# A GINE layer loop in which the adjacency is built in turns, the node chain has empty steps, and the edge weights have one buffer

## The chip, the core and the metric

The kernel runs on one core of a Trainium2 chip. The metric is device time in microseconds (us) from the start to the end of one launch; shown is the median of several runs. Engines: PE multiplies matrices (PEld is its weight load), DVE and ACT do elementwise work, POOL issues the indirect gathers, SP issues most other DMAs. Each engine runs its instructions in order.

## What is computed

A network of four graph layers, each followed by a feed-forward layer, on 1875 nodes with 256 features. The change touches the first graph layer, GINE, which itself has four layers:

```python
def _gine(x, src, dst, edge_attr, W1, b1, W2, b2, eW, eb, eps):
    e = edge_attr @ eW + eb
    m = jax.nn.relu(x[src] + e)
    agg = jax.ops.segment_sum(m, dst, num_segments=N)
    h = (1.0 + eps) * x + agg
    return jax.nn.relu(h @ W1 + b1) @ W2 + b2
...
h = _gine(x, src, dst, edge_attr, W1[0], ...)
for k in range(1, L):
    y = jax.nn.relu(_layernorm(h, gamma[k], beta[k]))
    h = h + _gine(y, src, dst, edge_attr, W1[k], ...)
return jax.nn.relu(_layernorm(h, gamma[0], beta[0]))
```

There are 31875 edges, sorted by destination. While GINE runs, the kernel also builds the weighted adjacency matrix that a later graph layer (the third) multiplies with.

## The kernel before, in words

Nodes lie in 15 tiles of 128. The edges of a tile are a window of 18 columns of 128 edges (the last tile: 12). Two columns make an **item**, so there are 9 items per tile, 6 in tile 14, 132 per layer and 528 in all; they are numbered 0 to 527, and g131 below is the DVE addition of item 131.

For each item `fast_gine` records: two gathers of source rows by POOL (`gather`, L1081); the edge product on PE (`edges`, L572, into one of four PSUM banks, with the weights `ew`); the membership matrix s on DVE (`members`, L579); the addition of the product to the gathered rows on DVE and the relu on ACT (`messages`, L587 and L588); and two products s x m that add up a tile's sum on PE (`sums`, L601). Gathers are recorded 9 items ahead of the sums, edge products 5, messages 2. Gathers cannot cross into the next layer, since they read the table `qt` that the node chains of the layer write.

The **node chain** of a finished tile (`fast_gine_node`) is a generator in pieces: z on DVE (L691); two transposes on PE (L700); zT on ACT (L702); the product with W1 on PE (L708); uT on ACT (L712); the product with W2 on PE (L717); x, its statistics and the root (L721 to L729); the reciprocal, scale and relu (L1139 to L737); and the row of the next table with its DMA (L743, L744). One piece of each open chain is recorded per item (`node_work`), two per item in tile 14. With the last item of a layer all open chains are run to their end, and then the chain of tile 14 is recorded in one go, with some steps of the adjacency between its pieces (the tuple `more`). Only when its row has landed can the next layer's gathers start.

The **adjacency** is also a generator. The edges are in 120 groups of 16 destinations, three products each, two groups to a pair, so 60 pairs and 360 products. A product needs a one-hot `row` and a weighted one-hot `col` from DVE (L371, L374); its sum `padj` is in one PSUM bank (L378). A copy on ACT (L381) moves a pair's result to `adj_stage`, and every fourth pair SP writes that out (L385). `advance` takes one step; a credit `due` grows by `rate` per item from item 66 on, in tiles 0 to 12. `group_columns` prepares the columns of a third of the groups at three tiles; it first brings the adjacency to the end of a pair.

`gine_weights` loads the weights of a layer into a pool of two buffers, the next layer's at tile 2. `group_loads` and `prepare_experts` are chores, one per item; they bring POOL the iotas f2own and f3own, each followed by a memset on DVE (L1614, L1616).

Almost all of this is recorded through `self.later`, which keeps the engines' instructions in the order of the program; some loads and memsets are free and are placed by the scheduler.

Of the kernel before, what the change touches and what calls it, by code (L numbers as in the profile page):

```python
# [94 lines left out]
class Net:  # L95
# [261 lines left out]
    def adjacency(self, pools):  # L357

        nc, pin = self.nc, self.later
        for pair in range(NG // 2):
            t, q = divmod(2 * pair, GP)
            if q == 0:
                self.adj_stage = pools["st"].tile([P, NT, P], F32, name="adj")
            pa = pools["ad"].tile([P, 2, GN * NT], F32, name="padj")
            for i in range(2):
                for u in range(GT):
                    c = (2 * pair + i) * GT + u
                    row = pools["r"].tile([P, P], F32, name="row")  # L370
                    pin(nc.vector.tensor_scalar(row, self.iota, self.grow[:, c:c + 1], None,  # L371
                                                op0=ALU.is_equal))
                    col = pools["c"].tile([P, GN * NT], F32, name="col")
                    pin(nc.vector.tensor_scalar(col, self.wide, self.gcol[:, c:c + 1],  # L374
                                                self.gwt[:, c:c + 1], op0=ALU.is_equal,
                                                op1=ALU.mult))
                    yield "rows"
                    pin(nc.tensor.matmul(pa[:, i, :], row, col, start=u == 0, stop=u == GT - 1))  # L378
                    if u < GT - 1 or i == 0:
                        yield "sum"  # L380
            pin(nc.scalar.copy(  # L381
                self.adj_stage[:, :, q * GN:(q + 2) * GN].rearrange("p a (i n) -> p i n a", i=2),
                pa.rearrange("p i (n a) -> p i n a", a=NT)))
            if q == GP - 2:
                nc.sync.dma_start(self.adj[t], self.adj_stage)  # L385
            yield "pair"

    def window_attrs(self, one, starts):
        nc = self.nc
# [90 lines left out]
    def fast_layer0_gnn(self):  # L480
        nc, tc, a = self.nc, self.tc, self.a
        with ExitStack() as ctx:
            one = ctx.enter_context(tc.tile_pool(name="q1", bufs=1))
            wp = ctx.enter_context(tc.tile_pool(name="qw", bufs=2))
            y = one.tile([P, NT, D], F32, name="y")
            self.adj = self.dram.tile([NT, P, NT, P], F32, name="adj")
            self.wide = one.tile([P, GN * NT], F32, name="wide")
            nc.gpsimd.iota(self.wide, pattern=[[1, GN * NT]], base=0, channel_multiplier=0,
                           allow_small_or_imprecise_dtypes=True)
            h = one.tile([P, NT, D], F32, name="hres")  # L490
            tables = [self.dram.tile([NP, D], F32, name=f"qt{l}") for l in range(4)]
            ebs = []
            for l in range(4):
                ebs.append(self.vector_row(one, a["L0_gnn_eb"][l], f"eb{l}"))
            with tc.tile_pool(name="qn", bufs=1) as sb:
                self.layernorm(y, self.x, sb)
                t0 = sb.tile([P, NT, D], F32, name="tab0")
                nc.vector.tensor_tensor(t0, y, ebs[0][:, None, :].to_broadcast([P, NT, D]),
                                        ALU.add)
                nc.sync.dma_start(by_tile(tables[0]), t0)  # L500
            starts = self.windows()
            w = self.gine_weights(0, wp)
            pools = {
                "g": ctx.enter_context(tc.tile_pool(name="qg", bufs=10)),
                "m": ctx.enter_context(tc.tile_pool(name="qm", bufs=4)),
                "s": ctx.enter_context(tc.tile_pool(name="qs", bufs=4)),
                "r": ctx.enter_context(tc.tile_pool(name="qr", bufs=4)),
                "e": ctx.enter_context(tc.tile_pool(name="qe", bufs=2)),
                "pe": ctx.enter_context(tc.tile_pool(name="qp", bufs=1, space=PSUM)),
                "pa": ctx.enter_context(tc.tile_pool(name="qa", bufs=2, space=PSUM)),  # L510
                "mm": ctx.enter_context(tc.tile_pool(name="qx", bufs=1, space=PSUM)),
                "ad": ctx.enter_context(tc.tile_pool(name="qd", bufs=1, space=PSUM)),
                "st": ctx.enter_context(tc.tile_pool(name="qt", bufs=1)),
                "c": ctx.enter_context(tc.tile_pool(name="qc", bufs=4)),
            }
            self.window_attrs(one, starts)
            with tc.tile_pool(name="gc", bufs=1) as sb:
                self.group_rows(one, sb, pools["ad"])
            pools["gc"] = ctx.enter_context(tc.tile_pool(name="gk", bufs=1))
            self.fast_gine(y, h, tables, ebs, w, wp, pools)  # L520

    def gine_weights(self, l, wp):
        nc, a = self.nc, self.a
        nxt = (l + 1) % 4
        w = {
            "w1": self.weight(wp, a["L0_gnn_W1"][l], "w1"),
            "w2": self.weight(wp, a["L0_gnn_W2"][l], "w2"),
            "b1": self.vector_col(wp, a["L0_gnn_b1"][l], D, "b1"),
            "b2": self.vector_row(wp, a["L0_gnn_b2"][l], "b2"),
            "eps": self.vector_row(wp, a["L0_gnn_eps"][l:l + 1], "eps", 1),  # L530
            "gam": self.vector_row(wp, a["L0_gnn_gamma"][nxt], "gam"),
            "bet": self.vector_row(wp, a["L0_gnn_beta"][nxt], "bet"),
        }
        nc.vector.tensor_scalar(w["eps"], w["eps"], 1.0, None, op0=ALU.add)

        ew = wp.tile([P, 4, D], F32, name="ew")
        nc.vector.memset(ew, 0.0)
        for i in range(4):
            nc.sync.dma_start(ew[i * ED:(i + 1) * ED, i, :], a["L0_gnn_eW"][l])
        w["ew"] = ew  # L540
        return w

    def fast_gine(self, y, h, tables, ebs, w, wp, pools):

# [21 lines left out]
        def edges(q):  # L566
            l, t, k = items[q]
            i = k % 4 if k < 8 else t % 4
            at = self.attr[:, t, k // 4 * 2:] if k < 8 else self.tail[:, t // 4]
            pes[q] = pools["pe"].tile([P, 2, D], F32, name=f"pe{q % 4}")  # L570
            for v in range(2):
                pin(nc.tensor.matmul(pes[q][:, v, :], at[:, v, :], ws[l]["ew"][:, i, :],  # L572
                                     start=True, stop=True))

        def members(q):
# [31 lines left out]
        state = {"g": 0, "m": 0, "e": 0, "at": "pair", "due": 0.0}  # L607


        FIRST, BETWEEN = 66, 22  # L610
        shares = [q >= FIRST and t < NT - 2 for q, (l, t, k) in enumerate(items)]
        rate = (2 * NG * GT - 3 * BETWEEN) / sum(shares) + 0.01

        def advance():
            if state["at"]:
# [12 lines left out]
                messages(state["m"])  # L628
                state["m"] += 1

        def multiplied(to):

            while state["e"] < min(to, total, state["m"] + 4):
                edges(state["e"])
                state["e"] += 1

        multiplied(AHEAD)
        made(MADE, 0)
        multiplied(AHEAD)
        nodes = []  # L640

        def node_work(pieces=1):
# [6 lines left out]
        for q, (l, t, k) in enumerate(items):  # L649
# [9 lines left out]
            end = sums(q)  # L659
            last = end and t == NT - 1  # L660
            if last:
                node_work(99)
                node = self.fast_gine_node(l, t, accs.pop(t), y, h, tables, ebs, ws[l], pools)
                more = (0, 2, 0, 4, 0, 0, 0, 0, 16) if l < 3 else ()
                for n, _ in itertools.zip_longest(more, node):
                    for _ in range(n or 0):
                        advance()
            multiplied(q + 1 + AHEAD)
            gathers(q + 1 + GATHERS, l + 1 if last else l)
            made(q + 1 + MADE, l + 1 if last else l)  # L670
            state["due"] += rate * shares[q]
# [10 lines left out]
    def fast_gine_node(self, l, t, acc, y, h, tables, ebs, w, pools):  # L682


        nc, pin = self.nc, self.later
        sb, ps = pools["e"], pools["mm"]
        if l == 0:
            pin(nc.vector.tensor_scalar(self.deg[:, t:t + 1], acc[:, D:D + 1], 1.0, None,
                                        op0=ALU.add))
# [9 lines left out]
        for c in range(KD):  # L699
            pin(nc.tensor.transpose(pz[:, c, :], z[:, c * P:(c + 1) * P], self.ident))  # L700
        yield True
        pin(nc.scalar.copy(zT, pz))  # L702
        yield True
        p1 = ps.tile([P, KD, P], F32, name="mm")
        uT = sb.tile([P, KD, P], F32, name="uT")
        for m in range(KD):
            for kc in range(KD):
                pin(nc.tensor.matmul(p1[:, m, :], w["w1"][:, kc, m * P:(m + 1) * P], zT[:, kc, :],  # L708
                                     start=kc == 0, stop=kc == KD - 1))
        yield True  # L710
        for m in range(KD):
            pin(nc.scalar.activation(uT[:, m, :], p1[:, m, :], AF.Relu, bias=w["b1"][:, m:m + 1]))  # L712
        yield True
# [2 lines left out]
        for kc in range(KD):  # L716
            pin(nc.tensor.matmul(p2, uT[:, kc, :], w["w2"][:, kc, :], start=kc == 0,  # L717
                                 stop=kc == KD - 1))
        yield True
        x = h[:, t, :]  # L720
        pin(nc.vector.tensor_tensor(x, skip if l else w["b2"], p2, ALU.add))  # L721
# [1416 lines left out]
```

## Time and profile before

| | us |
|---|---|
| median of 7 runs | 3782.39 (3777.95 to 3785.62) |
| the profiled execution | 3781.21 |
| its span in the profile | 3779.4 |
| GINE: first gather starts | 69.35 |
| GINE: x of the last tile done | 1513.83 |
| busy over the span: PE, DVE, ACT, POOL | 2923.5, 1836.3, 885.0, 1528.8 |

How to read it: busy times are of the whole span, so they mix eight layers with different limits. The page's groups give, for a line of the kernel, an engine and an operation, how often it ran, the busy time, the mean of one, and the idle time of the engine just before with what ended it. "issue" there means that the profile shows nothing that the engine waited for. The timeline gives start, duration, engine, line, operation, output and inputs, and in brackets the idle time before and its end. Ends of matmuls are modelled.

### The profile page before, as it was taken

The page shows a single profiled execution, that of the slowest core. Times are in us where ns is not written, and L with a number is a line of the kernel's source. Part 1 is how long each engine was busy: PE and PEld are TensorE (multiplying, and loading weights), DVE is VectorE, ACT ScalarE, POOL GpSimd, SP SyncE. Part 2 cuts the span into 40 slices and gives each one's busy share as a digit, 9 for nine tenths or more (in the row PEclk, how much of TensorE's full clock was granted, in tenths as well). Part 3 has the DMA queues.
Part 4 walks back from the last instruction along what each step waited for, and adds up shares of the span by engine and source line. Part 5 has one row for each costly group of instructions (what it writes and reads, how often), then busy time and mean ns, then how long its engine had stood idle before and what let it go on. Part 6 is the DMA issues. An engine that isn't in the chain of part 4 may idle for free. (4 is left out here: it accounts for less than half of the span.)

```text
span 3779.4 us, 42835 instructions
## 1 busy us (share of the span) xinstructions
PE 2923.5 (77%) x14099; PEld 2406.4 (64%) x14099; DVE 1836.3 (49%) x4981; ACT 885.0 (23%) x1933; POOL 1528.8 (40%) x1537
## 2 busy tenths in 40 slices
PE   3878789989987998679456565939967999686992
PEld 2667678868776876457344454728855888574772
DVE  5556567757766775861357661061251111442224
ACT  1333233323332333213111110200111222011220
POOL 2777477757775776000578721020003111003220
PEclk9989899999999999789667666969977999886996
DMA  5435685434443333015444413412004554503663
GB/s 150 123 112 178 177 190 131 120 106 120 120 120 105 113 113 99 24 52 158 123 132 139 132 54 118 138 71 114 1 8 165 176 168 143 200 1 126 187 193 104
DMA packets 302412, 453.64 MB, mean 120 GB/s; under 512 B 91737, under 2 KB 230436, under 8 KB 300388
## 3 DMA queue, kind: packets, MB, share of 16 engines
q1 hardware_dynamic: 226324, 248.21, 21.0%
q0 software_dynamic: 72672, 199.68, 18.4%
q10 hardware_dynamic: 3184, 2.91, 0.2%
q8 instruction: 114, 1.87, 0.2%
q14 instruction: 118, 0.97, 0.1%
HBM read 363.11 MB, written 87.56 MB: 119 GB/s over the span
## 5 line engine op out<-in xcount | busy, mean ns | idle before, releaser
L1081 POOL DMA_INDIRECT g<-qt,w_src x1056 | 1026.6, 972 | 416.1 <-issue 306.4
L601 PE MATMUL acc<-m,s 128*128 128x256 f32 (+1 forms) x2112 | 555.0, 386 | 8.7 <-ACT m L588 8.7
L587 DVE TENSOR_TENSOR g<-g,pe 128x512 f32<-128x512 f32 x528 | 361.5, 685 | 340.0 <-DMA g<-qt,w_src 336.3
L572 PE MATMUL pe<-ew,w_attr 128*128 128x256 f32 x1888 | 497.1, 387 | 31.2 <-DVE g L587 22.4
L588 ACT ACTIVATE m<-g 128x512 f32<-128x512 f32 x528 | 333.1, 631 | 753.0 <-DVE g L587 467.2
L1081 POOL DMA_INDIRECT g<-rq_h,w_tsrc x264 | 301.3, 1141 | 390.7 <-PE pz L859 310.9
L601 PEld LDWEIGHTS acc<-m,s 128*128 128x128 f32 x2112 | 400.5, 195 | 56.7 <-ACT m L588 10.6
L572 PEld LDWEIGHTS pe<-ew,w_attr 128*128 128x128 f32 x1888 | 360.1, 194 | 102.3 <-PE acc L601 37.4
L1087 POOL DMA_INDIRECT f_outs<-ye,token x104 | 99.7, 959 | 508.7 <-DVE ye L1772 502.5
L996 PE MATMUL acc<-h,adj 128*128 128x256 f32 x1350 | 294.7, 379 | 0.0
L1763 PE MATMUL hid<-xeT,w 128*128 128x256 f32 x1184 | 272.4, 387 | 24.3 <-DVE xeT L1758 22.7
L378 PE MATMUL padj<-col,row 128*128 128x240 f32 x720 | 218.3, 392 | 84.7 <-DVE col L374 77.2
L996 PEld LDWEIGHTS acc<-h,adj 128*128 128x128 f32 x1350 | 255.6, 190 | 33.6
L1087 POOL DMA_INDIRECT f_slots<-rows,slot x60 | 57.6, 961 | 515.5 <-DVE sl L1698 301.8
L1769 PE MATMUL out<-w,hidT 128*128 128x256 f32 x1184 | 264.0, 379 | 0.0
L1763 PEld LDWEIGHTS hid<-xeT,w 128*128 128x128 f32 x1184 | 222.3, 193 | 63.2 <-DVE xeT L1758 31.5
L1765 ACT ACTIVATE hidT<-hid,cols 128x256 f32<-128x256 f32 x296 | 138.2, 473 | 459.4 <-PE hid L1763 459.4
L1769 PEld LDWEIGHTS out<-w,hidT 128*128 128x128 f32 x1184 | 225.4, 190 | 30.1
L579 DVE TENSOR_TENSOR s<-iota,w_dst 128x256 f32<-128x256 f32 x528 | 221.6, 420 | 20.5 <-PE acc L601 20.4
L378 PEld LDWEIGHTS padj<-col,row 128*128 128x128 f32 x720 | 135.3, 198 | 131.7 <-DVE col L374 83.7
L1772 DVE TENSOR_SCALAR ye<-out,xe 128x256 f32<-128x256 f32 x104 | 50.3, 484 | 253.7 <-PE out L1769 253.7
L374 DVE TENSOR_SCALAR col<-wide,g_col,g_wt 128x240 f32<-128x240 f32 x360 | 148.1, 411 | 0.0
(388 smaller groups left out, 3736.5 us busy)
## 6 DMA issues: line engine op xcount, KB each, us to landing
w<-in_L_ffn_W SPq DMA_DIRECT2D x44, 1024.0 KB
adj<-adj SPq DMA_DIRECT2D x45, 960.0 KB
w<-in_L_ffn_w SPq DMA_DIRECT2D x60, 512.0 KB
w<-in_L_ffn_w SPq DMA_DIRECT2D x18, 1024.0 KB
g<-qt,w_src POOLq DMA_INDIRECT x1056, 2.8
dstrow<-lin SPq DMA_DIRECT2D x14, 1152.0 KB
rq_h<-hr SPq DMA_DIRECT2D x8, 1980.0 KB
xe<-f_slots SPq DMA_DIRECT2D x52, 258.0 KB
```

The source lines that it names most:

```text
L374: pin(nc.vector.tensor_scalar(col, self.wide, self.gcol[:, c:c + 1], self.gwt[:, c:c + 1], op0=ALU.is_equal, op1=ALU.mult))
L378: pin(nc.tensor.matmul(pa[:, i, :], row, col, start=u == 0, stop=u == GT - 1))
L572: pin(nc.tensor.matmul(pes[q][:, v, :], at[:, v, :], ws[l]["ew"][:, i, :], start=True, stop=True))
L579: pin(nc.vector.tensor_tensor(ss[q], self.iota[:, None, :].to_broadcast([P, 2, P]), self.wdst[:, c:c + 2, None].to_broadcast([P, 2, P]), A ...
L587: pin(nc.vector.tensor_tensor(g, g, pes.pop(q), ALU.add))
L588: pin(nc.scalar.activation(m[:, :, :D], g, AF.Relu))
L601: pin(nc.tensor.matmul(accs[t], s[:, v, :], m[:, v, :], start=k == v == 0, stop=end and v == 1))
L996: nc.tensor.matmul(acc, adj[t][:, u, :], h[:, u, :], start=u == 0, stop=u == NT - 1)
L1081: self.nc.gpsimd.indirect_dma_start(out=out, out_offset=None, in_=table, in_offset=bass.IndirectOffsetOnAxis(ap=at, axis=0))
L1087: return self.nc.gpsimd.indirect_dma_start(out=table, out_offset=bass.IndirectOffsetOnAxis(ap=at, axis=0), in_=in_, in_offset=None, **kw)
L1763: nc.tensor.matmul(p1, w1[:, kc, m * P:(m + 1) * P], xT[:, kc, :], start=kc == 0, stop=kc == KD - 1)
L1769: nc.tensor.matmul(p2, hT[:, m, i * P:(i + 1) * P], w2[:, m, :], start=m == 0, stop=m == fc - 1)
```

## The change

The adjacency is written as a list of turns: per pair six products, a copy, and an empty turn (None). A step of the generator is now one turn. In turn n the row and column for turn n+2 are recorded first, then the product, the copy, or nothing. So rows and columns are two turns ahead of their product, and the copy stands in a turn of its own behind the sixth product. A step was half of that before (rows and column, or product), so `BETWEEN` falls from 22 to 11 and `rate` is worked out from 8 turns a pair.

The node chain has four empty pieces: ahead of z, ahead of zT, ahead of uT, and ahead of x. It has 13 pieces instead of 9, and the tuple `more` follows.

The edge weights `ew` lie in one buffer for all layers instead of one of two; it is set to zero once, the next layer's weights are loaded with the last item of a layer, and edge products no longer cross into the next layer ahead of its start. The pools of messages (`qm`) and membership matrices (`qs`) have 5 and 6 buffers instead of 4 each.

```diff
 def adjacency(self, pools):
+        def rows(i):
+            row = pools["r"].tile([P, P], F32, name="row")
+            pin(nc.vector.tensor_scalar(row, self.iota, self.grow[:, i:i + 1], None,
+                                        op0=ALU.is_equal))
+            col = pools["c"].tile([P, GN * NT], F32, name="col")
+            pin(nc.vector.tensor_scalar(col, self.wide, self.gcol[:, i:i + 1], self.gwt[:, i:i + 1],
+                                        op0=ALU.is_equal, op1=ALU.mult))
+            sides[i] = row, col
+        turns = []
         for pair in range(NG // 2):
...
+            turns += [(pair, u) for u in range(2 * GT)] + [(pair, "copy"), None]
+        for n, turn in enumerate(turns):
+            for m in (0, 1, 2) if n == 0 else (n + 2,):
+                if m < len(turns) and turns[m] and turns[m][1] != "copy":
+                    rows(turns[m][0] * 2 * GT + turns[m][1])
+            if turn:
...
+                if u == "copy":
...
+                    pin(nc.scalar.copy(
...
+                    row, col = sides.pop(pair * 2 * GT + u)
+                    pin(nc.tensor.matmul(pa[:, u // GT, :], row, col, start=u % GT == 0,
+                                         stop=u % GT == GT - 1))
+            yield "sum" if turn else "pair"
 def fast_layer0_gnn(self):
+            self.ew = one.tile([P, 4, D], F32, name="ew")
+            nc.vector.memset(self.ew, 0.0)
+            self.edge_weights(0)
...
-                "m": ctx.enter_context(tc.tile_pool(name="qm", bufs=4)),
-                "s": ctx.enter_context(tc.tile_pool(name="qs", bufs=4)),
+                "m": ctx.enter_context(tc.tile_pool(name="qm", bufs=5)),
+                "s": ctx.enter_context(tc.tile_pool(name="qs", bufs=6)),
 def gine_weights(self, l, wp):
-        ew = wp.tile([P, 4, D], F32, name="ew")
-        nc.vector.memset(ew, 0.0)
+    def edge_weights(self, l):
         for i in range(4):
-            nc.sync.dma_start(ew[i * ED:(i + 1) * ED, i, :], a["L0_gnn_eW"][l])
+            self.nc.sync.dma_start(self.ew[i * ED:(i + 1) * ED, i, :], self.a["L0_gnn_eW"][l])
 def fast_gine(...):
-        FIRST, BETWEEN = 66, 22
+        FIRST, BETWEEN = 66, 11
-        rate = (2 * NG * GT - 3 * BETWEEN) / sum(shares) + 0.01
+        rate = (NG // 2 * (2 * GT + 2) - 3 * BETWEEN) / sum(shares) + 0.01
-            while state["e"] < min(to, total, state["m"] + 4):
+            while state["e"] < min(to, total, state["m"] + 4) and items[state["e"]][0] <= layer:
...
             if last:
+                if l < 3:
+                    self.edge_weights(l + 1)
                 node_work(99)
...
-                more = (0, 2, 0, 4, 0, 0, 0, 0, 16) if l < 3 else ()
+                more = (0, 0, 1, 0, 0, 2, 0, 0, 0, 0, 0, 0, 8) if l < 3 else ()
...
-            multiplied(q + 1 + AHEAD)
+            multiplied(q + 1 + AHEAD, l + 1 if last else l)
 def fast_gine_node(...):
+        yield True
...
```

In the last function `yield True` is added ahead of z, between the transposes and zT, between the product with W1 and uT, and between the product with W2 and x.

## Prediction

> **What bounds the kernel.** I read, in this order: the page's costliest groups, who POOL waits for, a table of busy time in stretches of 30 us, and the timeline at the ends of GINE's four layers. The change touches this stage alone (its first gather starts at 69.35 us, its last tile is done at 1513.83 us of a span of 3779.4). Columns of the groups: busy us, mean ns of one | idle us before them and what ended most of it.
>
> ```profile
> L1081 POOL DMA_INDIRECT g<-qt,w_src x1056 | 1026.6, 972 | 416.1 <-issue 306.4
> ...
> L378 PE MATMUL padj<-col,row 128*128 128x240 f32 x720 | 218.3, 392 | 84.7 <-DVE col L374 77.2
> ```
>
> A gather takes 0.972 us and 0.30 us pass before the next: 1056 x 1.27 = 1343 us of a stage of 1444. The wait list of the gathers agrees: apart from that gap (306.4 us in 940 cases) only `DMA qt<-row` stops POOL for long, twice for 55.1 us together. The stretches (us, then busy us and count of PE, PEld, DVE, ACT, POOL, clock, DMA share, GB/s) show the trap:
>
> ```profile
> 540.00:570.00 30.00, 30.00 (x151) 26.87 (x150) 21.66 (x62) 11.08 (x22) 22.69 (x25) 1.00 0.42 110
> ...
> 960.00:990.00 30.00, 28.38 (x136) 24.41 (x135) 22.58 (x67) 11.05 (x21) 22.69 (x25) 1.00 0.46 143
> ```
>
> PE is busy all the time and POOL for 22.7 of 30 us, but the 25 gathers with 25 gaps of 0.30 us fill POOL's 30 us. PE is full because it lags and catches up. The gather of item i+10 waits for the ACT pass (L588) of item i; by the timeline there are usually 20 us between the two, and the least is 0.4 us (item 144: pass ends 496.1, gather 496.5). So inside a layer POOL is never held, whatever PE waits for. POOL stands only where one layer's table must be complete before the next layer's first gather:
>
> ```profile
> 405.87 0.63 POOL L1614 IOTA f2own<- 128x88 f32 x1
> 439.22 1.22 POOL L1081 DMA_INDIRECT g<-qt,w_src  x1 [32.73 <-DMA qt<-row]
> ...
> 777.16 0.94 POOL L1081 DMA_INDIRECT g<-qt,w_src  x1 [0.30 <-issue]
> 800.46 0.94 POOL L1081 DMA_INDIRECT g<-qt,w_src  x1 [22.35 <-DMA qt<-row]
> ...
> 1135.84 0.95 POOL L1081 DMA_INDIRECT g<-qt,w_src  x1 [0.30 <-issue]
> 1157.68 0.94 POOL L1081 DMA_INDIRECT g<-qt,w_src  x1 [20.90 <-issue]
> ```
>
> The stage is thus four runs of gathers (336.5, 338.9, 336.3, 338.0 us) and four tails: 33.4, 22.4, 20.9, and 18.1 us from the last gather's end (1495.70) to x of tile 14 (1513.83); together 1444.5. A change gains or loses in the tails, or not at all.
>
> How a tail runs, in layer 1's (P1, P2: products with W1, W2, L708 and L717; x: L721; z: L691):
>
> ```profile
> 780.92 0.69 DVE L587 TENSOR_TENSOR g<-g,pe 128x512 f32<-128x512 f32 x1 [1.97 <-DMA g<-qt,w_src]
> ...
> 781.77 0.91 DVE L537 MEMSET ew<- 128x1024 f32 x1 [0.16 <-DVE g L587]
> ...
> 782.60 0.36 DVE L721 TENSOR_TENSOR hres<-skip,mm 128x256 f32<-128x256 f32 x1
> ...
> 786.77 0.48 DVE L691 SCALAR_TENSOR_TENSOR z<-y,eps,acc 128x256 f32<-128x256 f32 x1
> ...
> 790.16 0.96 ACT L381 COPY adj<-padj 128x480 f32<-128x480 f32 x1 [2.00 <-PE padj L378]
> ...
> 792.76 0.42 DVE L721 TENSOR_TENSOR hres<-skip,mm 128x256 f32<-128x256 f32 x1 [2.03 <-PE mm L717]
> ```
>
> The last message is added at 780.92. Then DVE ends **tile 13's** chain (x at 782.60 to its row), and only behind it, in order, comes z of tile 14 at 786.77, though its last sum ended at 785.34. From z to x takes 5.99 us, from x to the next gather 7.7.
>
> **Part by part.**
>
> *Adjacency in turns.* No instruction is added: 360 rows, 360 columns, 720 matmul records, 60 copies stay. PE's waits for columns (161.0 us before matmul and weight load, 115 times) and for copies (23.5) should go. Price 0: the gathers hide them. Were that cover not there, 184.5 us would be the most to win.
>
> *Buffers for messages and members.* s waits 20.4 us for sums; same cover, 0.
>
> *Edge weights in one buffer.* Three memsets (0.91 us) go; the one at 781.77 stands just before x (its gain is in the sums below, which count from the old times). A layer's four ew loads stay four, but now wait for the old layer's last edge product (about 413 in layer 0), with SP's later issues behind them; the row of tile 14 is due over 15 us after that, so nothing. New: the next layer's first four edge products stand on PE behind the tail, not before it. They take 4 x 0.86 = 3.4 us (twice that if slow); the first gathered pair lands 1.25 + 0.95 + 2.8 = 5.0 us after its gather starts, and a delay beyond that meets the 20 us of slack. Price 0; without that cover up to 2 us at each of three boundaries.
>
> *Empty steps.* The chain of a tile has 13 pieces instead of 9. In tile 14 two run per item, over five items and a flush. So before, tile 13's P2 stands behind the third-last sum (PE order P2, sum 261, 262, 263) and tile 12's chain is over; after, P2 stands behind sum 262, x and all behind it in the flush, and tile 12's x and row lie between DVE's last additions. With the rows of the trace, layer 1:
> - g260 772.45, x to ve of tile 12 1.25 us, z and skip of 13 0.9, g261 775.5 (data at 775.32), rs, y, relu, row of 12 3.3 us to 778.85, g262 779.15 (data 777.93), its ACT pass to 780.55, zT to 780.95.
> - P1 of 13 1.0 start to start, sums 261 and 262 0.86 each, P2 1.13: ends 784.8; x 784.85, and x to z is as before (786.77 - 782.60 = 4.2): z at 789.05, **+2.3**.
> - PE is idle from 776.1 (sum 260) to 780.95. After gaps of 5.77 and 7.35 us PE began slow (407.78: 2.04 us instead of 1.03; 449.98: 2.08), and at 1494.34 P1 took 2.07 instead of 1.16 after 1.83 us. With P1 and the next sum at that pace 1.45 more: **+3.75**.
>
> The same sum gives +3.75 or +5.2 for layer 2 (data at 1131.46, 1133.69, 1136.43, 1139.53; z was at 1144.36) and +2.55 or +4.2 for layer 3 (1490.07 to 1498.36; z was at 1504.09, and P1 was slow there already).
> In layer 0, worked out in the same way, DVE waits 12.19 us for POOL's f2own iota, queued behind the layer's last gather, and is let go at 406.57, with 8 additions left; after with 6 (the memset is in front of g126), and no next-layer edge products on PE. But P2 of 12 and 13 hang on ACT passes behind it: P2(12) ends 410.9, z(13) 412.7, row(12) 415.5, g131 417.4, zT(13) 417.7, P1 418.9, two sums, P2(13) 421.35, x 421.4, z 4.3 later: 425.7. Before: 425.69. **0**: what the shorter queue gains goes into tile 13's chain.
>
> *The copy's place in the tail.* Before, a copy (0.96 us) stood on ACT between zT and uT in layers 1 and 2: z to x 5.99 and 6.39 us against 4.47 in layer 0 without one. After, the instruction order has it in layer 0 alone. There it starts when the product behind P1 ends, 0.45 us after P1, and uT 0.77 us later (as 790.16 and 790.93 show) instead of 0.03 after P1: **+1.2**; in layers 1 and 2 **-1.5** and **-1.9**. In layer 0 SP issued the last row 0.5 us late behind gam and bet, which now stand behind it: **-0.5**.
>
> *POOL's pace.* 170 gathers take over 0.99 us; over 0.946 all take 29.0 us more, 5.8 to 8.5 a layer, in step with what DVE does beside them. DVE's work stays and shifts: bounds +-5 (four times about half that spread), value 0.
>
> **Sum**, PE slow at the start of P1(13): 0 + 1.2 - 0.5 + (3.75 - 1.5) + (5.2 - 1.9) + 4.2 = **+10.4 us**; at full pace 5.9. I take the first, since the gaps (4.7 to 4.9 us) lie nearer 5.77 than the gaps that began at full pace (787.31: 1.97). If the last chain's P1 and P2 run slow too (PE idles some 4 us before z), 1.85 us more in each tail, 7.4 at most.
>
> [...]
>
> The profiled execution took 3781.21 us (1.8 around its span), 1.2 below the median of 7: 3781.2 + 10.4 + 1.2 = 3792.8; I say **3792.5**.
>
> **Rivals.**
> 1. *Nothing to measure*, within 0.2% (7.6 us, about what a measurement of this kernel can tell): PE starts P1(13) at full pace (+5.9), or POOL's pace gives some back: 3775 to 3790, most likely 3788. For it: at 1132.59 PE took the usual 0.44 us after 2.03 idle. 0.31.
> 2. *Faster*: tile 13's chain does not hold z of tile 14, because its P2 ends over 4.2 us before the last sum of tile 14. Then layer 0's tail wins (two additions and five edge products fewer behind the f2own wait: last ACT pass 418.3, sum 419.3, against 425.7: -6.4), the copies' 0.7 - 1.5 - 1.9 count in full, and the other z stay: -9.1, 3773.7. Against it: PE's order has P2(13) directly before that last sum. 0.07.
> 3. *PE was the bound*, so that its waits count: up to -184, 3598. Against: POOL's gaps of 0.30 us. 0.02.
> 4. *POOL held at item 144*, where the slack was 0.4 us: two more rows are flushed there. But PE no longer waits for the column at 481.88, and ends sum 140 earlier. Some 5 us more, 3797. 0.05.
> 5. *The change does not do what it says*: the order has rows two products ahead, so it does; no gain follows.
>
> Forecast 0.55. Slower 0.55 + 0.05 = 0.60, same 0.31, faster 0.07 + 0.02 = 0.09. The range: upwards all chains slow and POOL 5 us worse, 10.4 + 7.4 + 5 = 22.8 over 3782.4, 3805; downwards rival 1's lower part, 3776, where rival 2 begins.
>
> **What would show it.** Runs of gathers at 336 to 339 us each (else POOL's pace or rival 4); PE's waits for columns and copies near none while the stage does not shorten; tails near 34.1, 24.6, 24.2 and 22.3 us; tile 14's z directly behind tile 13's row; P1 of tile 13 near 2 us. A tail of layer 0 under 29 us, or tails 1 to 3 not longer, would prove it wrong.

## The result, and the profile after

The changed kernel takes 3794.66 us (median of 13 runs) where the kernel before takes 3782.39 (33 runs): a ratio of 1.0033, 95% interval 1.0026 to 1.0040, or 12.3 us more. The forecast was 3792.5 us.

Three groups of the page of the changed kernel answer to those shown before (busy us, mean ns of one | idle us before them and what ended most of it):

```profile
L1101 POOL DMA_INDIRECT g<-qt,w_src x1056 | 1024.4, 970 | 428.5 <-issue 346.0
...
L396 PE MATMUL padj<-col,row 128*128 128x240 f32 x720 | 207.5, 384 | 15.7 <-DVE col L369 12.8
...
L396 PEld LDWEIGHTS padj<-col,row 128*128 128x128 f32 x720 | 142.2, 200 | 38.4 <-ACT adj L386 10.5
```

The weight loads of the kernel before:

```profile
L378 PEld LDWEIGHTS padj<-col,row 128*128 128x128 f32 x720 | 135.3, 198 | 131.7 <-DVE col L374 83.7
```

The change did what it says: PE's idle time ahead of the adjacency products fell from 84.7 to 15.7 us, that ahead of their weight loads from 131.7 to 38.4. The two overlap and must not be added: the time in which neither ran fell from 84.2 to 15.6 us. The gathers did not notice: 1024.4 us busy instead of 1026.6, and 12 us more idle.

The idle time is in the tails, as the timeline of POOL in the changed kernel shows:

```profile
405.10 0.63 POOL L1634 IOTA f2own<- 128x88 f32 x1
439.30 0.96 POOL L1101 DMA_INDIRECT g<-qt,w_src  x1 [33.56 <-DMA qt<-row]
...
806.44 0.94 POOL L1101 DMA_INDIRECT g<-qt,w_src  x1 [27.39 <-issue]
...
1169.81 0.94 POOL L1101 DMA_INDIRECT g<-qt,w_src  x1 [26.63 <-issue]
```

With the end of the stage that makes the table below (us). z, x and next are the sections of a tail: from the last gather's end to the start of tile 14's z, from there to the end of its x, from there to the next gather (in layer 3, to the end of the tile's work).

| tail | before | after | more | z | x | next |
|---|---|---|---|---|---|---|
| layer 0 | 33.36 | 34.20 | +0.8 | +0.5 | +2.4 | -2.1 |
| layer 1 | 22.36 | 27.40 | +5.0 | +4.9 | 0.0 | +0.2 |
| layer 2 | 20.89 | 26.63 | +5.7 | +5.0 | +0.7 | +0.1 |
| layer 3 | 18.13 | 23.17 | +5.0 | +3.8 | +1.2 | +0.1 |
| sum | 94.74 | 111.40 | **+16.7** | +14.1 | +4.3 | -1.7 |

The four runs of gathers take 336.18, 339.74, 336.74 and 335.69 us, together 1.4 less than before; the first gather starts 0.4 earlier, and the unchanged code behind the stage took 3.9 us less in this execution. That makes 10.9 us between the two spans (3790.3 and 3779.4).

Layer 1's tail in the timeline of the changed kernel (its last gather ended at 779.04):

```profile
779.23 0.43 DVE L763 TENSOR_TENSOR row<-y,eb 128x256 f32<-128x256 f32 x1 [0.48 <-ACT y L757]
...
780.75 0.63 ACT L602 ACTIVATE m<-g 128x512 f32<-128x512 f32 x1 [1.55 <-DVE g L601]
781.28 0.35 ACT L720 COPY zT<-mm 128x256 f32<-128x256 f32 x1
781.69 2.08 PE L726 MATMUL mm<-zT,w 128*128 128x128 f32 x8 [4.61 <-ACT zT L720]
...
783.56 3.62 PE L615 MATMUL acc<-m,s 128*128 128x256 f32 x8
...
786.97 1.35 PE L736 MATMUL mm<-w,uT 128*128 128x256 f32 x4
...
788.36 0.42 DVE L741 TENSOR_TENSOR hres<-skip,mm 128x256 f32<-128x256 f32 x1 [5.59 <-PE mm L736]
...
792.25 0.43 DVE L763 TENSOR_TENSOR row<-y,eb 128x256 f32<-128x256 f32 x1 [0.48 <-ACT y L757]
792.59 0.47 DVE L708 SCALAR_TENSOR_TENSOR z<-y,eps,acc 128x256 f32<-128x256 f32 x1
...
793.12 0.44 PE L717 MATMUL mm<-ident,z 128*128 128x128 f32 x2 [3.93 <-DVE z L708]
...
794.02 1.71 PE L726 MATMUL mm<-zT,w 128*128 128x128 f32 x8
```

Tile 12's row (779.23) stands on DVE in front of the last additions; zT of tile 13 waits on ACT behind the pass of one of them (780.75); so P1 of tile 13 starts only at 781.69, after 4.61 us of idle PE, and takes 2.08 us; in the kernel before it took 1.16 (at 777.11). The two sums behind it take 1.81 each, where one took 1.03. P2 ends, x of tile 13 follows at 788.36, its row at 792.25, and directly behind it z of tile 14 at 792.59, 13.55 us after the last gather instead of 8.67. In the kernel before, too, z stood directly behind the end of tile 13's chain, but only 0.1 to 1.5 us after tile 14's last sum; now it is 3.4 to 3.5 us after it in all four layers, and in layers 1 to 3 that sum itself ends 1.8 to 2.9 us later after the last gather. Then PE has been idle for 3.93 us again, and P1 of tile 14 takes 1.71 instead of 1.05.

### The profile page after: what moved, and what is told of

The parts are those of the page before. It is cut to its first block, busy times and chain, and to the rows that moved or that the text cites. A ratio compares the mean times of both kernels' runs of the same rounds, so it can differ in the third digit from the quotient of the medians.

```text
span 3790.3 us, 42595 instructions
## 1 busy us (share of the span) xinstructions
PE 2930.8 (77%) x14099; PEld 2408.4 (64%) x14099; DVE 1830.5 (48%) x4978; ACT 884.7 (23%) x1933; POOL 1527.1 (40%) x1537
## 3 DMA queue, kind: packets, MB, share of 16 engines
q1 hardware_dynamic: 226324, 248.21, 20.9%
q0 software_dynamic: 72672, 199.68, 18.3%
## 5 line engine op out<-in xcount | busy, mean ns | idle before, releaser
L1101 POOL DMA_INDIRECT g<-qt,w_src x1056 | 1024.4, 970 | 428.5 <-issue 346.0
L396 PE MATMUL padj<-col,row 128*128 128x240 f32 x720 | 207.5, 384 | 15.7 <-DVE col L369 12.8
L396 PEld LDWEIGHTS padj<-col,row 128*128 128x128 f32 x720 | 142.2, 200 | 38.4 <-ACT adj L386 10.5
```

The costliest lines, as they stand in the source:

```text
L396: pin(nc.tensor.matmul(pa[:, u // GT, :], row, col, start=u % GT == 0, stop=u % GT == GT - 1))
L1101: self.nc.gpsimd.indirect_dma_start(out=out, out_offset=None, in_=table, in_offset=bass.IndirectOffsetOnAxis(ap=at, axis=0))
```

## The theories, and the chips

**T1**, the prediction's: only the tails count, and they grow because the longer chain puts tile 13's end in front of tile 14's z; the turns and buffers are worth nothing. **R1**: the edge products that are now held inside their layer leave PE idle and slow, and the steps cost nothing. **R2**: the turns, or the copy's new place, cost the time.

The experiments fell on five chips. On two of them (those of the runs e5, e6, e9, e1b and e3b) the kernel before took 3785.0 and 3783.6 us, about as in the result. On the other three it took 4180.3, 4220.1 and 4224.7 us. A stretch of 250 us inside layer 2 tells the two kinds apart; in the order of the columns: PE, PEld, DVE, ACT, POOL, granted clock, DMA share, GB/s. With the turns alone, on a chip of the first kind:

```profile
850.00:1100.00 250.00, 231.16 (x1090) 193.72 (x1089) 180.91 (x513) 88.15 (x164) 190.88 (x195) 1.00 0.41 120
```

and a kernel with the same node chain on one of the second (run e2b):

```profile
850.00:1100.00 250.00, 190.41 (x776) 154.90 (x775) 125.12 (x359) 62.25 (x119) 133.32 (x139) 0.86 0.30 89
```

139 gathers instead of 195: there the gathers do not set the pace, and a run of gathers takes 401 to 423 us instead of 336 to 340. What these seven runs say of tails is therefore not taken over to the others; they stand at the end, apart.

## Experiments on chips where the gathers set the pace

| kernel | turns, buffers | one buffer, edge products held | empty steps | tails 0 to 3, us | sum against before | ratio (95%) | us |
|---|---|---|---|---|---|---|---|
| before | | | | 33.4, 22.4, 20.9, 18.1 | | | |
| e5 | x | | | 33.2, 21.9, 18.9, 17.4 | -3.3 | 0.9983 (0.9974 to 0.9992) | -5.8 |
| e1b | | | x | 40.4, 30.5, 29.8, 23.3 | +29.3 | 1.0082 (1.0068 to 1.0096) | +28.7 |
| e3b | x | | x | 38.0, 30.0, 27.1, 23.6 | +23.9 | 1.0058 (1.0044 to 1.0072) | +21.8 |
| after | x | x | x | 34.2, 27.4, 26.6, 23.2 | +16.7 | 1.0033 (1.0026 to 1.0040) | +12.3 |
| e6 | x | x | x, PE kept busy | 34.1, 23.1, 21.9, 19.6 | +4.0 | 0.9998 (0.9989 to 1.0007) | -1.4 |
| e9 | x, memset moved | | | 25.7, 20.7, 19.0, 18.3 | -11.0 | 0.9960 (0.9946 to 0.9974) | -16.5 |

The last column is the difference of the medians. Tails come from one profiled execution each; their sums and the medians agree within 6 us.

**Turns and buffers alone (e5).** The kernel before with the new adjacency (as in the diff), five and six buffers, and the lists fitted to the longer count of turns:

```diff
-                more = (0, 2, 0, 4, 0, 0, 0, 0, 16) if l < 3 else ()
+                more = (0, 1, 0, 2, 0, 0, 0, 0, 8) if l < 3 else ()
```

> The kernel before with the adjacency in turns (rows two turns ahead, the copy one behind) and the added buffers for messages and members; the node chain of nine pieces and the edge weights stay as before. T1: PE's waits for columns go, but the gathers bound the layers, so nothing changes: a ratio of 0.999 to 1.001 on a chip that grants the clock in full inside the layers. On a chip that grants 0.8 there, where PE sets the pace, fewer waits of PE could show: 0.995 to 1.0. R2 (the turns and the copy's place cost the 12 us): a ratio of 1.003.

Measured 3779.21 us (11 runs) against 3785.01 (21 runs): 0.9983. R2 falls. So does T1's nothing: there is a small gain. 3.3 us of it are in the tails: x of tile 14 comes 1.9 us sooner in layer 2 (4.90 us after z instead of 6.81), where the copy no longer stands on ACT between zT and uT, and in layer 0 the next gather 2.0 us sooner after x, though z and x are later there. The rest shows in no section of the profile. PE's idle time did not go, it moved: in the whole stage it was 185 us in the kernel before and is 184 in e5. In e5 it is 15.9 us ahead of the adjacency products, like the 15.7 of the changed kernel, but ahead of the edge products it rose from 31.2 us to 79.9 (first the kernel before, then e5):

```profile
L572 PE MATMUL pe<-ew,w_attr 128*128 128x256 f32 x1888 | 497.1, 387 | 31.2 <-DVE g L587 22.4
...
L584 PE MATMUL pe<-ew,w_attr 128*128 128x256 f32 x1888 | 506.5, 392 | 79.9 <-DVE g L599 73.0
```

**PE kept busy in the tails (e6).** The changed kernel with products of the identity and a constant, written to an edge buffer that is free and read by nobody: nine of them behind the third sum of tile 14, eight behind the last. No other instruction moves.

```diff
             end = sums(q)
             last = end and t == NT - 1
+            if t == NT - 1 and (k == 2 or last):
+                filler(q, 9 if k == 2 else 8)
```

> The changed kernel with products that nobody reads on PE in each tail: nine of 128x240 behind the sum of the third item of tile 14 and eight behind the last sum, some 3.5 and 3.1 us, put where PE stood idle 4 to 5 us; the order of all else stays. It tells the clock's share from the order's share. T1: P1 of tile 13 takes 1.03 us instead of 2.07, and so do P1 and P2 of tile 14; about 1.0 to 1.45 us earlier z and 1.85 less to x in each tail, 6 to 11 us in all: 3784 to 3789 where the changed kernel takes 3794.7, the rest of the loss being the order alone. Rival: the filler delays P1 and the transposes by its own length or the pace does not depend on idle time: no change or slower than 3795.

Measured 3783.66 us (11 runs) against 3785.01: 0.9998, so 13 us less than the changed kernel by the two ratios, somewhat more than T1 had. Layer 1's tail in its timeline (last gather's end 780.33):

```profile
778.20 3.81 PE L648 MATMUL pe<-wide,ident 128*128 128x240 f32 x18
...
782.57 0.35 ACT L728 COPY zT<-mm 128x256 f32<-128x256 f32 x1
782.97 1.16 PE L734 MATMUL mm<-zT,w 128*128 128x128 f32 x8 [0.96 <-ACT zT L728]
...
783.97 1.89 PE L615 MATMUL acc<-m,s 128*128 128x256 f32 x8
...
785.70 1.03 PE L744 MATMUL mm<-w,uT 128*128 128x256 f32 x4
...
790.99 0.47 DVE L716 SCALAR_TENSOR_TENSOR z<-y,eps,acc 128x256 f32<-128x256 f32 x1
...
791.52 0.44 PE L725 MATMUL mm<-ident,z 128*128 128x128 f32 x2 [0.69 <-DVE z L716]
...
792.42 1.16 PE L734 MATMUL mm<-zT,w 128*128 128x128 f32 x8
```

The order is the same, z still follows tile 13's row, and P1 still waits for the same zT. But PE is idle for 0.96 and 0.69 us instead of 4.61 and 3.93, and P1, the two sums together and P2 take 1.16, 1.89 and 1.03 us instead of 2.08, 3.62 and 1.35. In layers 1 to 3 z comes 10.4 to 10.7 us after the last gather (layer 0: 21.5), and x is done 4.95 us after z (layer 0: 6.05). So of the 16.7 us of the changed kernel's tails 12.6 are the slow pace, and 4.0 are left for the order, the copy's place in it. All but 0.1 of the 12.6 is in layers 1 to 3. In layer 0 the filler run is no faster: ahead of the filler, which starts at 416.18, its products ran at half pace (four for a sum took 1.92 us at 411.38, and 1.03 at 414.22), and z is 1.2 us later than in the changed kernel, x 1.25 sooner after z.

The granted clock says the same. Stretches of layer 1's tail, changed kernel:

```profile
778.00:781.60 3.60, 0.00 (x0) 0.00 (x0) 2.41 (x6) 1.27 (x3) 1.00 (x1) 0.50 0.42 100
781.60:788.00 6.40, 6.31 (x20) 5.46 (x21) 0.69 (x1) 1.29 (x4) 0.00 (x0) 0.53 0.02 7
```

and with the filler:

```profile
778.00:781.60 3.60, 3.60 (x19) 3.37 (x18) 2.94 (x11) 1.05 (x2) 1.95 (x2) 1.00 0.33 91
781.60:788.00 6.40, 5.43 (x30) 4.62 (x29) 2.43 (x7) 2.04 (x5) 0.00 (x0) 1.00 0.11 31
```

**Edge products across layers (e3b).** The changed kernel, with two buffers of edge weights and the next layer's edge products multiplied in the tail again:

```diff
-            while state["e"] < min(to, total, state["m"] + 4) and items[state["e"]][0] <= layer:
+            while state["e"] < min(to, total, state["m"] + 4):
...
-                if l < 3:
-                    self.edge_weights(l + 1)
```

> The changed kernel with the edge weights in two buffers again and the next layer's edge products on PE in the tail, once more, on another chip. Against it stand the kernel with turns and buffers alone (5.8 us faster than before) and the changed kernel (12.3 slower): what is between the first and this is the empty steps with PE kept busy, what is between this and the second is the one buffer of edge weights. T1 as sharpened by the filler run (order 2 to 3 us in each of three tails, the slow pace some 3 us in each of four): 0 to +3 us against before, a ratio of 1.000 to 1.001. R1 (the one buffer alone is the cause): as turns and buffers alone, 0.998 to 0.999. The empty steps alone the cause, the buffer nothing: 1.003.

Measured 3805.35 us (5 runs) against 3783.57 (9 runs): 1.0058. All three expectations fell: with these products on PE the steps cost more, not less. The timeline of its layer 1 (last gather's end 783.14) shows why:

```profile
781.19 1.10 PE L585 MATMUL pe<-ew,w_attr 128*128 128x256 f32 x4
...
784.23 0.43 DVE L760 TENSOR_TENSOR row<-y,eb 128x256 f32<-128x256 f32 x1 [0.48 <-ACT y L754]
...
786.69 2.08 PE L723 MATMUL mm<-zT,w 128*128 128x128 f32 x8 [4.40 <-ACT zT L717]
...
788.56 1.91 PE L614 MATMUL acc<-m,s 128*128 128x256 f32 x4
...
790.27 1.34 PE L585 MATMUL pe<-ew,w_attr 128*128 128x256 f32 x4
791.45 1.03 PE L614 MATMUL acc<-m,s 128*128 128x256 f32 x4
792.31 1.03 PE L585 MATMUL pe<-ew,w_attr 128*128 128x256 f32 x4
793.17 1.03 PE L733 MATMUL mm<-w,uT 128*128 128x256 f32 x4
...
798.47 0.47 DVE L705 SCALAR_TENSOR_TENSOR z<-y,eps,acc 128x256 f32<-128x256 f32 x1
```

I had thought that these products would fill PE's gap. They can't: PE takes its work in program order, the one in front of P1 is done at 782.3, and the gap of 4.40 us is there all the same. The next two stand between P1 and P2 of tile 13 and push P2, x, the row and z back: P2 starts 6.48 us after P1, in the changed kernel 5.28. And the clearing of the second buffer (0.91 us) is on DVE in front of tile 12's row. R1 falls, and its opposite holds: beside the steps, the one buffer, with its products held and without the clearings, is a gain, 7.2 us of tails. What of it is the products and what the clearings was not tried apart.

**The empty steps alone (e1b).** Four lines `yield True` in the node chain of the kernel before, and the list fitted to 13 pieces.

> The kernel before with the four empty steps alone, once more, on another chip: the next layer's edge products still stand on PE in the tails. T1: z of tile 14 comes 2 to 3 us later in layers 1 to 3, PE at full pace, +6 to +9 us, a ratio of 1.0015 to 1.0025. R1: no change. The slow pace comes with the steps themselves, whatever PE has to do: +12 or more, 1.003.

Measured 3812.25 us (5 runs) against 3783.57: 1.0082, the third case of the expectation and beyond it. z of tile 14 comes 6.0, 6.2, 6.8 and 4.2 us later, x 2.2, 1.7, 2.1 and 0.9 later after it. Steps without turns and held products have the slow P1 (layer 1: 2.08 us after 4.40 us of idle PE), the two edge products between P1 and P2, and the copy between zT and uT in the last chain. R1 and R2 are out: the steps are the whole loss, and the other parts give more than half of it back.

**A better kernel (e9).** e5, and in `slot_rows` one line moved to POOL, behind the iota that it waited for on DVE:

```diff
-        nc.vector.memset(own[:, :, 0:1], 0.0)
+        self.later(nc.gpsimd.memset(own[:, :, 0:1], 0.0))
```

> Turns and buffers without the empty steps and with the edge weights as before, and the clearing of f2own and f3own moved from DVE to POOL behind its iota: the version that should beat both. T1: layer 0's tail, 33.2 us with DVE's wait, falls to 22 to 25 us, and the rest stays as in the run of turns and buffers alone: 3768 to 3772 where before takes 3785, a ratio of 0.9955 to 0.9965. Rival, that the backlog behind the wait is not what sets this tail: 0.998 to 0.999 as without the move.

Measured 3767.07 us (5 runs) against 3783.57: 0.9960, faster than both kernels of this case. On POOL, in e9's timeline:

```profile
407.53 0.95 POOL L1093 DMA_INDIRECT g<-qt,w_src  x1 [0.30 <-issue]
408.48 0.63 POOL L1626 IOTA f2own<- 128x88 f32 x1
409.17 0.14 POOL L1628 MEMSET f2own<- 128x44 f32 x1
434.22 0.97 POOL L1093 DMA_INDIRECT g<-qt,w_src  x1 [24.91 <-DMA qt<-row]
```

The iota still waits behind the layer's last gather, but DVE does not stand behind it any more: the last message is added 3.9 us after the last gather instead of 12.1, and layer 0's tail is 25.7 us. T1 held; the tail is just over its 22 to 25.

## Runs on the three other chips

Each is told by its ratio to the kernel before on the same chip. The edits of e1, e2 and e3 are those of e1b, e2b and e3b.

No empty steps, all else as changed (e2, e2b: nine pieces, and the list (0, 1, 0, 2, 0, 0, 0, 0, 8)):

> The changed kernel with the four empty steps taken out again (nine pieces, the turns beside the last chain spread as before), all else as changed. T1: the tails go back to about 33, 22, 20 and 18 us and the time to 3779 to 3785. R1: PE still has no edge products of the next layer in the tail, so the time stays at 3788 to 3795. R2: stays at 3792 to 3795.

> The changed kernel without the four empty steps, once more, on another chip: turns, buffers and the edge weights in one buffer. Turns and buffers alone gave 0.9983. If the edge products held inside their layer help by themselves (the changed kernel is 9.5 us faster than its like with the edge products let across): 0.995 to 0.997, 3765 to 3773. If they help only where tile 13's chain stands behind them on PE, as T1 now has it: 0.998 to 0.999, 3777 to 3783. If they leave PE idle and slow: over 1.000.

1.0004 (0.9984 to 1.0024) and 1.0008 (0.9984 to 1.0031): no difference from before. Steps alone, and the changed kernel with edge products let across:

> The kernel before with the four empty steps in the node chain alone (the list of adjacency turns beside the last chain is spread over 13 steps instead of 9); its adjacency, its buffers and its edge weights stay. Theory T1 (the longer chain puts tile 13's end in front of z of tile 14): z comes 2.3 to 3.75 us later after the last gather in layers 1 to 3, 0 to 4 us in layer 0; the next layer's edge products still stand on PE in the tail, so PE runs at full pace and the lower ends are likely: +6 to +9 us, 3788 to 3792. Rival R1 (the edge products held inside a layer are the cause, because PE goes idle and slow): within 2 us of before, 3782. Rival R2 (the turns and the copy's new place are the cause): 3782 as well.

> The changed kernel with the edge weights in two buffers again, and the edge products of the next layer multiplied in the tail as before. T1: z of tile 14 is as late as in the changed kernel but for the slow pace, some 1.5 us earlier, and the last chain runs at full pace, some 1.9 us less: 3 us less in three or four tails, 3783 to 3788, still over before. R1: back to 3782. R2: stays at 3792 to 3795.

1.0070 (1.0043 to 1.0096) and 1.0092 (1.0067 to 1.0118). Three pieces per item in tile 14, so that tile 13's chain of 13 pieces is over in time (`node_work(3 if t == NT - 1 else 1)`), twice:

> The changed kernel, but in tile 14's items three pieces of each open node chain run instead of two, so that tile 13's chain of 13 pieces is over before tile 14's last sum, as the chain of nine was. T1: z of tile 14 follows its last sum, 7.5 to 9 us after the last gather in layers 1 to 3, earlier than 20 us in layer 0: 3774 to 3784. R1: PE is as idle as in the changed kernel: 3788 to 3795. R2: 3792 to 3795.

> The changed kernel with three pieces of each open chain per item of tile 14 instead of two, once more, on another chip: the steps stay, but tile 13's chain of 13 pieces is over before tile 14's last sum. T1 (the steps cost only through tile 13's chain, which stands in front of z of tile 14): z 7.5 to 9 us after the last gather in layers 1 to 3, tails about 33, 22, 20 and 18 us, and the time of the kernel before or less: 3776 to 3785, a ratio of 0.998 to 1.000. Rival (the steps cost by themselves, wherever the chain ends): 1.002 to 1.003, as the changed kernel.

1.0048 (1.0031 to 1.0066) and 1.0018 (0.9999 to 1.0037). And the kernel before with the memset on POOL:

> The kernel before, with one line moved: the clearing of f2own and f3own stands on POOL, directly behind the iota that it waited for on DVE. In the kernel before DVE stood 12.19 us for f2own's iota at the end of layer 0 with the last eight additions behind it. Theory T1 (only the tails count): layer 0's tail, 33.4 us, falls to 22 to 25 us, the other tails stay at 22, 21 and 18 us: 3771 to 3775 where before takes 3782, a ratio of 0.997 to 0.998. A rival, that layer 0's tail is set by something else behind the wait (PE's backlog): no change.

1.0007 (0.9993 to 1.0021): no difference where POOL is not the limit; that the same line gives its gain on the first kind of chip, e9 shows.

So there too the steps are what costs, and without them nothing is lost. T1's tails could not be tried on these chips, but their order can be read: with three pieces z of tile 14 starts 1.7 us after its last sum in both runs, as in e2 and e2b without the steps, and not 3.4 us after it as in e1. The order was mended; why e4 still took 1.0048 of the time of the kernel before is not shown. Whether three pieces per item mend the changed kernel's time, and what holding the edge products is worth without the steps, stays open: both of their runs fell on chips of the second kind.

## Why the prediction was right, step by step

- *Bound by the gathers, tails alone count*: right. PE's waits for columns and copies nearly went, and the runs of gathers changed by 1.4 in sum. The 161.0 and 184.5 us of the working were too much, since they add the idle time of PE to that of its weight load; the time in which neither ran was 84.2 us in all. The least slack was not 0.4 us at item 144 but 0.27 at item 143. No gather was held there (now 2.0 and 0.6 us), so rival 4 did not come.
- *Empty steps, PE slow at P1(13)*: right in place and size. z of tile 14: 0, 3.75, 5.2 and 4.2 us predicted, 0.5, 4.9, 5.0 and 3.8 measured; P1(13) took 2.08, 2.08, 2.08 and 2.07 us. At full pace the working had 0, 2.3, 3.75 and 2.55; the run with the filler, which has that pace in layers 1 to 3, shows 1.7, 2.0, 2.8 and 2.3. Rival 2, that tile 13's chain does not hold z, fell with z directly behind the row and at least 3.4 us after its own last sum. (By its own terms that rival came to 3773.3 us, 3782.4 less 9.1, and not to 3773.7.)
- *Copy's place*: right at full pace, where the filler run has x 1.2 later after z in layer 0 and 1.5 and 1.9 sooner in layers 1 and 2, to the tenth as predicted; in layer 3 it is 0.9 sooner, where 0 was forecast, because P2 of the kernel before ran slow there (2.08 us). In the changed kernel none of that gain is seen.
- **The mis-sized term**: the last chain's slow pace, kept out of the sum as "1.85 us more in each tail, 7.4 at most". It came in all four: x after z is 2.4, 0.0, 0.7 and 1.2 us longer where 1.2, -1.5, -1.9 and 0 had been forecast, 6.5 us in sum. The reason to count it was in the working, PE idle for some 4 us before z, little less than the 4.7 to 4.9 for which P1(13) was taken as slow.
- *Layer 0's row*: -0.5 predicted, -2.1 measured. The issue came 0.5 sooner as said, and the row was there 2.6 us after it instead of 4.2, with the loads of gam and bet behind it (451.16 and 452.69).
- *Edge weights in one buffer, 0*, and *turns, 0*: not right as terms. The sum for the steps was worked out on a PE without the next layer's edge products and without the memset, so it held the buffer's gain of some 7 us of tails inside the step's loss; and the turns' parts in the tails were counted under the copy. Taken one by one the steps cost 28.7 us, the turns and buffers give 5.8, and the one buffer gives some 10 beside the steps (21.8 less 12.3). A reader who would undo one part must use these, not the prediction's.
- Why the time was hit to 2 us: the tails are 6.3 us longer than forecast, and 5.7 us came back outside them in the profile, 1.4 in the gathers, 0.4 ahead of them and 3.9 in code behind the stage that the change doesn't touch. The other profiled executions of the table differ by about as much there (2265.9 to 2269.6 us after the stage's last x), so this part is luck.
- *The slow start after 1.83 us* (1494.34): the granted clock of the kernel before fell at 1493.31, ahead of it, behind 3.41 us in which PE was busy for 1.30 (lines in the last section).

## What to carry to other kernels

In a stage that one engine paces, only the places where that engine stands are worth a look: PE's waits ahead of the adjacency products went, PE idled elsewhere instead, and turns and buffers together gave 6 us. There, read the order on each in-order engine: a chain that is cut into more pieces ends later, and all that stands behind its end is late by it (z in layer 1: 13.55 us after the last gather instead of 8.67); work that is put on an idle engine fills a gap only if it stands in the right place of its program order (in e3b the 4.40 us ahead of P1 stayed). And price idle time on PE in front of a critical chain as products that may be slow, at every such place and not only the first: here P1 took 1.71 to 2.08 us, twice in each tail, where it took 1.05 to 1.16 in e6. A few products that nobody reads, put exactly into the gap, can pay for themselves: in e6 they took 13 us off the changed kernel.

## What the runs showed of the hardware

- In the profiles of the kernel before and of the changed kernel the granted clock of PE is 1.00 or 0.50 and nothing between, and in each of the two all of its steps lie on one grid of 3.413 us. Cut along this grid, their stages show how busy PE was just ahead of a step or of none. In the kernel before it was busy for at most 0.47 of the time ahead of a fall (16 cases), and for at least 0.49 where the clock stayed up (369); in the changed kernel for at most 0.54 (17) and at least 0.43 (367). Ahead of a rise it was busy for at least 0.86 (15) and 0.93 (16), and where the clock stayed down for at most 0.81 (20) and 0.87 (19). (Ends of matmuls are modelled; these are the counts of two executions, not limits.) Here are PE's busy us and products, and the clock in the same stretch (then DMA share and GB/s), first in the changed kernel, then in the kernel before:

```profile
401.92:405.33 3.41, 1.46 (x7) 1.00 1.07 385
405.33:408.74 3.41, 1.94 (x8) 1.00 1.08 394
...
412.16:415.57 3.41, 0.60 (x3) 1.00 1.09 370
415.57:418.98 3.41, 3.17 (x12) 0.50 1.15 223
418.98:422.40 3.42, 2.98 (x14) 1.00 1.15 238
```

```profile
1489.90:1493.31 3.41, 1.30 (x6) 1.00 0.43 115
1493.31:1496.72 3.41, 2.38 (x10) 0.50 0.31 90
```

- A short gap was slow here and a longer one not. In the changed kernel's tails PE was slow at P1 of tile 13 (2.07 or 2.08 us) and in the chain of tile 14 (P1 of 1.71 to 2.08 us), eight places with 3.05 to 4.9 us of idle before them; but 3.24 us of idle before 406.62, which fall on the first two of the lines above, cost nothing (four products in 1.13 us). In the kernel before 1.83 us did, at 1494.34: PE had idled for 2.11 of the 3.41 us up to 1493.31, where the clock fell. After the 0.46 to 1.47 us of idle that the filler left, P1 took 1.05 to 1.16 us (seven of the eight chains) and P2 1.02 to 1.13.
- On the way up, the clock of the changed kernel rose 3.1 to 3.3 us after P1 of tile 13 began in layers 0, 2 and 3 (at 418.98, 1149.44 and 1511.25), and 5.9 us after it in layer 1 (787.62). In those three PE was busy for 3.10 to 3.33 of the 3.41 us before the rise; in layer 1 it was busy for 2.52 of the 3.41 in which P1 began, and the clock stayed down for 3.41 more.
- This program had different limits on different chips. On three of five the kernel took 10 to 12% longer, and DVE and ACT stood again and again inside the layers: between 100 and 400 us DVE did so 14 times for 5.1 to 13.0 us in e2b and ACT 13 times for 6.1 to 12.3, in the kernel before either one twice (DVE for 13.98 and 7.89). The granted clock inside the layers was 0.82 to 0.86 in the four profiles of e1, e2b, e4 and e4b, and 0.94 to 1.00 in the seven of the table. What held the engines is not shown. PE idles too (busy for 190.4 of 250 us in e2b, for 231.2 in e5), so the low clock may be the result of these stalls as well as their cause.
